# Two graph-network layers on one core: the residual sums of the output frame as two 512-wide operations behind the third clip, in place of four 256-wide ones between the second and the third

## The chip, the core and the metric

The kernel runs on one core of a Trainium2 chip. TensorE (PE) multiplies matrices, VectorE (DVE), ScalarE (ACT) and GpSimd (POOL) work on elements, SyncE (SP) starts most transfers; each has a queue of its own that it works off in order. The metric is the device time of one execution in microseconds (us), lower being better.

## The reference, cut to what matters

The input `x` holds 8 graphs of 2048 nodes with 256 features, in float32, and one 2048 x 2048 adjacency serves them all. Layer 0, which the change concerns, is

```python
h = jnp.maximum(_layernorm(x, axis=-1), 0.0)
q, k, v = h @ Wq.T + bq, h @ Wk.T + bk, h @ Wv.T + bv      # 4 heads of 64
scores = einsum('bhnd,bhjcd->bhnjc', q, kc) / sqrt(64)      # keys in 8 chunks of 256
scores = jnp.clip(scores, -10.0, 10.0)
scores = jnp.where(mask == 0, -10.0, scores)
attn = jax.nn.softmax(scores, axis=-1)                      # within each chunk
ctx = einsum('bhnjc,bhjcd->bhnd', attn, vc)                 # summed over chunks
out = ctx @ Wo.T + bo + h                                   # the residual sum
x = x + (layernorm(out) * gamma + beta)
```

Layer 1 is a graph attention layer on `relu(layernorm(x))`, with one softmax over all 2048 neighbours, and adds its relu to `x`. The change touches the line of the residual sum, `out = ctx @ Wo.T + bo + h`, and only the order and the shape in which its last addition is done.

## The kernel before, in words

**Tiling.** For each graph the queries are cut into 4 blocks of 512 (`NB`, index `nb`) and the keys into 8 chunks of 256 (`j`). A step of the attention is one pair (block, chunk): 32 steps a graph, 256 in all. Activations lie transposed, so a step's logits are [128 keys x 512 queries] tiles. The four heads are taken one after another in the order `ORDER`, index `o` from 0 to 3; heads that lie in the lower 64 rows of the array alternate with heads in the upper 64, so two half-arrays of 64 rows, each split into four column groups of 32, work side by side. Below they are called the two halves.

**The frame.** `begin(f)` and `end(f)` write out one frame, in which four steps overlap: the logits and clips of step f-1, most of the values and the sums of step f-2, the rest of the values, the inversion and the scaling of step f-3, and the first logits of step f. `logits` (L411) is the matrix product of keys and queries; `clip` (L451, DVE) reads a pair of banks of logits, clips them and applies the mask in one operation, and so frees the pair; `exponentials` (L460) is on ACT; `values` (L427) and `sums` (L439) are PE again; `scale` (L481, DVE) multiplies by the inverse sum into `prod`, and `gather` (L486, POOL) adds `prod` to `ctxT` by an accumulating DMA. The clips of o = 0 to 3 are called the first to the fourth; the first is in `begin`, the others in `end`.

**What sets the order.** `tc.manual_schedule` takes the order of the program as it is written, so an engine's queue is the order in which the Python calls are made. Between engines, semaphores hold back readers and writers of the same buffer. In PSUM there are two double banks `ps_s` for logits, two banks `ps_n` for values and two banks `ps_t`, taken in turns. So `logits(f-1, 3, ...)` needs the pair that the second clip of the same frame has freed, and `logits(f, 0, 0)` the pair that the third has freed.

**Work beside the attention.** `Between.beside` hands out the rest of the layer as pieces with a half-frame number n; even n go to `begin`, odd n to `end`. A piece has a kind that says where in the frame it is called. The pieces of the output projection of a finished block are at n = 8 and n = 9, that is, in one frame, which is called the output frame below. In `begin`, `output_tiled(0)` (kind `pe`) puts 32 matmul calls of 256 columns ahead of the logits of the second and third heads, and in `end` `output_tiled(1)` (kind `pe1`, L635) puts another 32 behind them. Together they fill two `ps_t` banks, `pp[0]` and `pp[1]`. The addition of the residual, `ps_t` plus `hn0` into `o4`, is then `take_tiles` (L650, kind `mid`): for i = 0 and 1 it adds 256 columns out of each of the two banks. `end` runs these pieces after the second clip and before the third. The bank `pp[0]` is then taken again by `sums(f-2, 1)` in the same frame. Pieces without a kind that belong to n = 8, among them `stats([0])` on `o4`, run after the third clip. There are 3 such blocks for each of 8 graphs, so 24 output frames; the fourth block of a graph takes another way (`output`, and `take` at L658).

**Two fp32 passes.** Each fp32 matmul call is recorded as two instructions: the logits make 256 x 4 x 2 x 4 = 8192 calls, and the profile counts 16384.

Of the kernel before, what the change touches and what calls it, by code (L numbers as in the profile page):

```python
# [8 lines left out]
F32 = mybir.dt.float32  # L9
# [4 lines left out]
ALU = mybir.AluOpType  # L14
# [3 lines left out]
P = 128  # L18
# [10 lines left out]
def gnn_two_layers(  # L29
# [18 lines left out]
    nc = tc.nc  # L48
    B, N, F = x.shape
# [6 lines left out]
    TB = NB // P  # L56
    NNB = N // NB
# [36 lines left out]
    work = ctx.enter_context(tc.tile_pool(name="work", bufs=2, reuse_waits="tile"))  # L94
# [64 lines left out]
    def first(piece):  # L159

        piece.kind = "first"
        return piece

    def pe(piece):

        piece.kind = "pe"
        return piece

    def pe1(piece):
        piece.kind = "pe1"  # L170
        return piece

    def mid_clips(piece):
        piece.kind = "mid"
        return piece


# [105 lines left out]
    def norm_tiles(tag, bufs):  # L283
        mv = small.tile([P, TB, 2], F32, tag="mv", name="mv")
        rn = small.tile([P, 2, TB], F32, tag=tag, name=tag, bufs=bufs)
        return mv, rn
# [94 lines left out]
    def fence(before, after):  # L381

        nop = nc.sync.nop()  # L383
        for x in before:
            tc.add_manual_dep(nop.ins, x.ins.name, SYNC, reason="both write one bank of PSUM")
        for x in after:
            tc.add_manual_dep(x.ins, nop.ins.name, SYNC, reason="both write one bank of PSUM")


    class Attention:  # L390
# [159 lines left out]
        def end(self, f, pieces=()):  # L550
            self.run(pieces, "first")
            if self.has(f - 1):
                self.clip(f - 1, 1)
            self.run(pieces, "pe1")
            self.run(pieces, "mid")
            if self.has(f - 1):
                self.clip(f - 1, 2)
            self.run(self.rest, None)
            if self.has(f - 1):
                self.exponentials(f - 1, 1)  # L560
                self.exponentials(f - 1, 2)
            if self.has(f - 2):
                made = {}
                for kt in range(KT):
                    for half, c in ((0, 1), (1, 0)):
                        made.setdefault(c, []).extend(self.values(f - 2, half, c, kt))
                for c in range(2):
                    self.before[f - 2, c] = made[c]
            if self.has(f - 1):
                self.logits(f - 1, 3, 0)  # L570
            if self.has(f - 2):
                sums = self.sums(f - 2, 1)
            if self.has(f - 1):
                self.logits(f - 1, 3, 1)
            if self.has(f):
                self.logits(f, 0, 0)
            self.run(pieces, None)
            self.run(pieces, "pe")
            if self.has(f - 2):
                fence(sums, self.sums(f - 2, 0))  # L580
            if self.has(f):
                self.logits(f, 0, 1)
            if self.has(f - 1):
                self.clip(f - 1, 3)
                self.add(f - 1, 0)
# [8 lines left out]
    class Between:  # L594
# [23 lines left out]
        def output_tiled(self, turn):  # L618
# [22 lines left out]
            for t2 in range(2) if turn else ():  # L641
                fence(self.made[t2], made[t2])
            self.made = made

        def take_tiles(self, i):
            if i == 0:
                self.o4 = work.tile([P, TB, F], F32, tag="o4", name="o4", bufs=1)
                self.mv, self.rn = norm_tiles("rn", 2 * NNB)
            for t2 in range(2):
                nc.vector.tensor_tensor(  # L650
                    self.o4[:, 2 * t2 + i, :], self.pp[t2][:, i * F:(i + 1) * F], self.hn0[t2][:, i, :], op=ALU.add
                )

        def take(self, t2):
            if t2 == 0:
# [90 lines left out]
        def beside(self):  # L746

            todo = {
                -3: [self.load],
                3: [lambda: self.residual(0)],  # L750
                4: [lambda: self.residual(1)],
                5: [lambda: self.bias(0)],
                6: [lambda: self.bias(1)],
                8: [pe(lambda: self.output_tiled(0)), lambda: self.stats([0]), lambda: self.beta(0)],
                9: [
                    pe1(lambda: self.output_tiled(1)), mid_clips(lambda: self.take_tiles(0)),
                    mid_clips(lambda: self.take_tiles(1)), lambda: self.stats([1]),
                ],
                10: [lambda: self.stats([2]), lambda: self.beta(1)],
                11: [lambda: self.stats([3])],  # L760
                12: [self.power],
                13: [self.shift],
                14: [lambda: self.scaled(range(TB))],
                15: [lambda: self.gamma(0)],
                16: [lambda: self.gamma(1)],
                18: [lambda: self.add(0)],
                20: [lambda: self.add(1)],
            }

            def at(n, *pieces):  # L770
                todo.setdefault(n, []).extend(pieces)

            if self.nb == NNB - 2:
                return todo
            at(22, lambda: self.stats1([0]))

            at(25, first(lambda: self.stats1([1, 2, 3])))
            at(26, self.power1)
            at(27, self.shift1)
            if self.nb == 1:  # L780
                at(28, lambda: self.norm1(0))
                at(29, lambda: self.norm1(1))
            return todo
# [225 lines left out]
    for b in range(B):  # L1009
# [3 lines left out]
        zero, low, mid, last = blocks  # L1013
# [271 lines left out]
```

The softmax here doesn't subtract the row's maximum and nothing guards it: scores larger than these inputs give would overflow.

## Time and profile before

| | |
|---|---|
| median of 3 runs | 3626.41 us (3624.73 to 3626.59) |
| the profiled execution's own time | 3624.46 us |
| its span | 3622.7 us |
| PE busy, by the page | 3587.4 us, 99% of the span |
| DVE busy | 2580.6 us, 71% |
| ACT busy | 1960.9 us, 54% |
| POOL busy | 1788.1 us, 49% |
| `take_tiles`, L650 on DVE | 96 operations, 34.0 us |
| granted TensorE clock | 0.998 |

Busy times are unions of the instructions of an engine. The ends of matmuls are modelled in the profile and not recorded, so PE's share says that matmuls were in flight and not that PE never waited; starts are recorded. PEld is the weight load of PE. In the lists of groups, the number after the bar is the busy time in us and the mean of one in ns, then the idle time of the engine just ahead of the group with what ended most of it. In a timeline, each row gives the start, the length, the engine, the line, the operation, the tiles, how many operations were merged into the row, and in brackets the idle time ahead of it.

### The profile page before, as it was taken

The numbers are of one execution on the slowest core, as the hardware profiler recorded it, in microseconds if no ns is written. First come the engines' busy times: TensorE is split into PE (matmuls) and PEld (weight loads), VectorE is DVE, ScalarE is ACT, GpSimd is POOL, SyncE is SP. The second block draws the span as 40 slices with busy tenths as digits, with TensorE's granted clock in tenths as the row PEclk, the third lists the DMA queues.
The fourth block names the chain that finished last, engine by engine and source line by source line (L and its number), as shares of the span: only waits on it lengthen the run. The fifth ranks groups of instructions, "written<-read, shape, count | busy, mean of one in ns | idle before, by whom it ended". The sixth has DMA issues, their size and how long they took to land.

```text
span 3622.7 us, 104823 instructions
## 1 busy us (share of the span) xinstructions
PE 3587.4 (99%) x46544; PEld 2202.7 (61%) x46544; DVE 2580.6 (71%) x3967; ACT 1960.9 (54%) x2975; POOL 1788.1 (49%) x1138
## 2 busy tenths in 40 slices
PE   8999999999999999999999999999999999999999
PEld 4444785547744577555775558744586455865568
DVE  5887577866777667786677766677576785757866
ACT  5677416774167732676326772367723677137650
POOL 0678016870178702786027850378503784047831
PEclk9999999999999999999999999999999999999999
DMA  6444213341133412343113432144322343114321
GB/s 223 114 109 100 49 56 84 84 107 35 64 81 83 107 35 68 84 96 83 53 50 84 104 74 62 48 85 99 71 61 59 78 96 73 53 48 92 75 60 44
DMA packets 149431, 283.62 MB, mean 78 GB/s; under 512 B 39664, under 2 KB 104944, under 8 KB 140784
## 3 DMA queue, kind: packets, MB, share of 16 engines
q0 software_dynamic: 32256, 117.45, 17.6%
q1 hardware_dynamic: 100080, 157.36, 13.5%
q8 instruction: 364, 5.96, 0.7%
q10 hardware_dynamic: 16640, 2.10, 0.4%
q14 instruction: 91, 0.75, 0.1%
HBM read 138.41 MB, written 21.02 MB: 44 GB/s over the span
## 4 chain that ended last, share of the span: by engine, by line
PE 96%; DMA 2%; ACT 1%; DVE 1%; issue 0%; POOL 0%; ACTq 0%; SPq 0%; DVEq 0%; POOLq 0%
PE ps_s L411 24%; PE ps_n L427 24%; PE ps_s L865 12%; PE ps_t L439 6%; PE ps_n L865 6%; PE ps_t L865 6%; PE ps_t L635 2%; PE ps_t L355 2%; PE ps_n L355 2%; PE ps_s L355 2%; PE ps_t L723 2%; PE ps_n L723 1%; PE ps_t L369 1%; PE ps_n L369 1%; PE ps_t L302 1%; DMA ctxT<-prod 1%
## 5 line engine op out<-in xcount | busy, mean ns | idle before, releaser
L466 POOL TENSOR_TENSOR both<-e 128x1024 f32<-128x1024 f32 x512 | 1217.8, 2406 | 641.1 <-PE ps_t L439 353.3
L451 DVE SCALAR_TENSOR_TENSOR e<-ps_s,bound 128x1024 f32<-128x1024 f32 x1024 | 1223.9, 1220 | 401.4 <-PE ps_s L411 398.6
L411 PE MATMUL ps_s<-q,k 64*32 64x512 f32 x16384 | 1435.0, 590 | 2.1 <-DVE e L451 2.1
L460 ACT ACTIVATE e<-e 128x1024 f32<-128x1024 f32 x1024 | 1050.5, 1050 | 524.8 <-DVE e L451 505.1
L427 PE MATMUL ps_n<-e,v 64*32 64x512 f32 x16384 | 1220.2, 590 | 2.7 <-ACT e L460 2.1
L427 PEld LDWEIGHTS ps_n<-e,v 64*32 64x32 f32 x16384 | 453.9, 107 | 476.4 <-issue 396.4
L411 PEld LDWEIGHTS ps_s<-q,k 64*32 64x32 f32 x16384 | 451.8, 106 | 472.0 <-issue 326.9
L883 POOL TENSOR_TENSOR x<-x,r 128x256 f32<-128x256 f32 x124 | 95.8, 773 | 1107.2 <-DVE rz L875 1000.7
L439 PE MATMUL ps_t<-both,ones 64*32 64x512 f32 x4096 | 534.7, 591 | 0.1
L865 PE MATMUL ps_s<-g,w 128*128 128x257 f32 x2048 | 448.5, 380 | 0.0
L865 PEld LDWEIGHTS ps_s<-g,w 128*128 128x128 f32 x2048 | 389.4, 190 | 56.5
L481 DVE TENSOR_TENSOR prod<-ps_n,rz 128x512 f32<-128x512 f32 x448 | 288.3, 685 | 159.3 <-PE ps_n L427 96.4
L848 DVE SCALAR_TENSOR_TENSOR w<-bound,w 128x1024 f32<-128x1024 int8 x256 | 313.7, 1225 | 8.7
L865 PE MATMUL ps_n<-g,w 128*128 128x257 f32 x1024 | 292.4, 382 | 0.0
L865 PE MATMUL ps_t<-g,w 128*128 128x257 f32 x1024 | 289.8, 380 | 0.0
L842 DVE TENSOR_SCALAR w<-src,cd 128x512 f32<-128x512 f32 x512 | 265.2, 560 | 10.7 <-ACT src L836 6.9
L471 ACT ACTIVATE rz<-ps_t 128x512 f32<-128x512 f32 x256 | 152.8, 597 | 175.7 <-PE ps_t L439 136.9
L486 POOL DMA_DIRECT2D ctxT<-prod x224 | 192.3, 859 | 57.7 <-DVE prod L481 55.2
L865 PEld LDWEIGHTS ps_n<-g,w 128*128 128x128 f32 x1024 | 192.8, 190 | 44.3 <-issue 17.6
L865 PEld LDWEIGHTS ps_t<-g,w 128*128 128x128 f32 x1024 | 193.8, 189 | 28.2
L275 ACT ACTIVATE krn<-mv,eps 128x4 f32<-128x4 f32 x32 | 9.5, 296 | 292.7 <-DVE mv L271 292.7
L439 PEld LDWEIGHTS ps_t<-both,ones 64*32 64x32 f32 x4096 | 115.2, 106 | 85.8 <-SPq L383 42.4
(126 smaller groups left out, 3005.0 us busy)
## 6 DMA issues: line engine op xcount, KB each, us to landing
ctxT<-prod POOLq DMA_DIRECT2D x224, 512.0 KB, 4.8
bound<-bound_d SPq DMA_DIRECT2D x62, 1024.0 KB, 5.7
xp<-in_x_dram SPq DMA_DIRECT2D x60, 512.0 KB, 5.7
rows<-in_adj_dram SPq DMA_DIRECT2D x32, 512.0 KB, 5.2
x<-in_x_dram SPq DMA_DIRECT2D x32, 512.0 KB, 4.6
out_dram<-x SPq DMA_DIRECT2D x31, 512.0 KB, 2.9
src<-source_d SPq DMA_DIRECT2D x24, 256.0 KB, 4.8
bound_d<-bound_part ACTq DMA_DIRECT2D x16, 128.0 KB, 4.4
```

The costliest lines, as they stand in the source:

```text
L355: nc.tensor.matmul(pp, w[:, di, do * P:(do + 1) * P], self.hT[nb][:, di, :], start=di == 0, stop=di == FC - 1,)
L411: nc.tensor.matmul(self.s[n, o][c * Q:(c + 1) * Q, kt, :], self.k[p][rows, at:at + Q], self.q[p][rows, nb * NB:(nb + 1) * NB], start=True, ...
L427: made.append(nc.tensor.matmul(self.num[n, c][h * Q:(h + 1) * Q, :], self.v[rows, j * KT + kt, at:at + Q], self.e[n, p][rows, i * KT + kt, :],
L439: nc.tensor.matmul(self.total[n][h * Q:(h + 1) * Q, :], ones[rows, :], self.both[n, h // 2][rows, h % 2, :], start=half == 1, stop=half == 0,)
L451: nc.vector.scalar_tensor_tensor(self.e[n, p][:, i * KT:(i + 1) * KT, :], self.s.pop((n, o)), -CLIP * SC, bounds[nb][:, j * KT:(j + 1) * K ...
L460: nc.scalar.activation(e, e, AF.Exp, scale=1.0 / SC)
L466: nc.gpsimd.tensor_tensor(self.both[n, p], e[:, 0], e[:, 1], op=ALU.add)
L481: nc.vector.tensor_tensor(dst[:, c, :], self.num.pop((n, c)), self.rz[n], op=ALU.mult)
L486: nc.gpsimd.dma_start(self.ctxT[nb], self.prod.pop(n), accum_op=ALU.add)
L842: nc.vector.tensor_scalar(w[:, i, :], self.src[nb], self.cd[:, 0, j:j + 1], self.cd[:, 1, j:j + 1], op0=ALU.mult, op1=ALU.max,)
L848: nc.vector.scalar_tensor_tensor(two, bounds1[nb][:, j - 1:j + 1, :], 0.0, two, op0=ALU.is_gt, op1=ALU.mult)
L865: nc.tensor.matmul(accs[t][:, 0:F + 1], w[:, i, t * P:(t + 1) * P], g[:, j, :], start=j == 0, stop=j == NT - 1,)
```

## The change

The four 256-wide additions between the second and the third clip become two 512-wide ones, one for each bank, and they are called after the third clip. The method `take`, which the last block of a graph used already, does them; `take_tiles` goes. Matmuls, banks, ACT, POOL and SP keep their work and their order.

```diff
-    def mid_clips(piece):
-        piece.kind = "mid"
+    def after_clips(piece):
+        piece.kind = "after"
         return piece
...
             self.run(pieces, "pe1")
-            self.run(pieces, "mid")
             if self.has(f - 1):
                 self.clip(f - 1, 2)
+            self.run(pieces, "after")
             self.run(self.rest, None)
...
-        def take_tiles(self, i):
-            if i == 0:
-                self.o4 = work.tile([P, TB, F], F32, tag="o4", name="o4", bufs=1)
-                self.mv, self.rn = norm_tiles("rn", 2 * NNB)
-            for t2 in range(2):
-                nc.vector.tensor_tensor(
-                    self.o4[:, 2 * t2 + i, :], self.pp[t2][:, i * F:(i + 1) * F], self.hn0[t2][:, i, :], op=ALU.add
-                )
-
...
                 9: [
-                    pe1(lambda: self.output_tiled(1)), mid_clips(lambda: self.take_tiles(0)),
-                    mid_clips(lambda: self.take_tiles(1)), lambda: self.stats([1]),
+                    pe1(lambda: self.output_tiled(1)), after_clips(lambda: self.take(0)),
+                    after_clips(lambda: self.take(1)), lambda: self.stats([1]),
                 ],
```

The method that is now called in the output frame, unchanged:

```python
        def take(self, t2):
            if t2 == 0:
                self.o4 = work.tile([P, TB, F], F32, tag="o4", name="o4", bufs=1)
                self.mv, self.rn = norm_tiles("rn", 2 * NNB)
            nc.vector.tensor_tensor(
                self.o4[:, 2 * t2:2 * t2 + 2, :], self.pp[t2].rearrange("p (i f) -> p i f", i=2),
                self.hn0[t2], op=ALU.add,
            )
```

## The prediction

> **What bounds the kernel now.** First the page, for the shares of the engines.
>
> ```profile
> PE 3587.4 (99%) x46544; PEld 2202.7 (61%) x46544; DVE 2580.6 (71%) x3967; ACT 1960.9 (54%) x2975; POOL 1788.1 (49%) x1138
> ```
>
> PE bounds it and no other engine is near. But the ends of matmuls are modelled, so a short stall of PE shows only in its starts. Second, the groups of DVE with their shapes kept apart, for the operation that goes and the one that comes.
>
> ```profile
> L650 DVE TENSOR_TENSOR o<-ps_t,hn 128x256 f32<-128x256 f32 x96 | 34.0, 416 | 26.0 <-PE ps_t L635 26.0
> ...
> L658 DVE TENSOR_TENSOR o<-ps_t,hn 128x512 f32<-128x512 f32 x8 | 5.5, 690 | 12.1 <-PE ps_t L613 12.1
> ```
>
> L650 is `take_tiles`: DVE stands idle ahead of it for 26.0/24 = 1.1 us in each output frame, until the last output matmul is done. L658 is `take`, as the fourth block runs it. Third, the timeline of DVE through the output frame of graph 0, block 1.
>
> ```profile
> 249.29 1.23 DVE L451 SCALAR_TENSOR_TENSOR e<-ps_s,bound 128x1024 f32<-128x1024 f32 x1 [0.49 <-PE ps_s L411]
> 251.62 1.42 DVE L650 TENSOR_TENSOR o<-ps_t,hn 128x256 f32<-128x256 f32 x4 [1.10 <-PE ps_t L635]
> 252.95 1.21 DVE L451 SCALAR_TENSOR_TENSOR e<-ps_s,bound 128x1024 f32<-128x1024 f32 x1
> ```
>
> The rows are the second clip, the four additions and the third clip, which ends at 254.16. It stands behind the 1.10 us of idleness and the 1.42 us of additions only because DVE's queue is in that order. Fourth, PE in the same stretch.
>
> ```profile
> 253.01 0.61 PE L439 MATMUL ps_t<-both,ones 64*32 64x512 f32 x4
> 253.34 0.62 PE L411 MATMUL ps_s<-q,k 64*32 64x512 f32 x4
> ...
> 253.44 0.61 PE L439 MATMUL ps_t<-both,ones 64*32 64x512 f32 x4
> 253.77 1.08 PE L411 MATMUL ps_s<-q,k 64*32 64x512 f32 x8
> ...
> 254.22 0.13 PEld L411 LDWEIGHTS ps_s<-q,k 64*32 64x32 f32 x5 [0.73 <-DVE e L451]
> ```
>
> Each row x4 fills the four column groups of one half; within a half the next follows 0.43 us later. The half that did sums at 253.01 and 253.44 is due with `logits(f, 0, 0)` at 253.87. It starts at 254.22, 0.06 us after the third clip's end, and its weight load names that clip: 0.35 us lost. Is it made up? The starts of the first sums of four successive frames answer that.
>
> ```profile
> 241.84 0.61 PE L439 MATMUL ps_t<-both,ones 64*32 64x512 f32 x4
> ...
> 253.01 0.61 PE L439 MATMUL ps_t<-both,ones 64*32 64x512 f32 x4
> ...
> 261.11 0.61 PE L439 MATMUL ps_t<-both,ones 64*32 64x512 f32 x4
> ...
> 268.83 0.61 PE L439 MATMUL ps_t<-both,ones 64*32 64x512 f32 x4
> ```
>
> The distances are 11.17, 8.10 and 7.72. An undisturbed frame takes 7.725 (9 groups in each half, two passes each, 18 x 0.429). The output matmuls add 16 groups of 256 columns in each half, 16 x 0.215 = 3.43, so 11.16 is due for the first distance, and 0.02 is lost there. The second has no matmul beyond a plain frame's and is 8.093 by the trace's unrounded starts: 0.368 lost for good. In all 21 output frames of graphs 1 to 7, and in this one, the loss lies between 0.367 and 0.369.
>
> **What the Trainium skill says.** "Perfetto Trace Analysis", Identifying the Most-Contended Engine: the busy share of matmuls is no good measure of PE's headroom. The trace agrees: the page's 99% contain the 0.368. "TensorE: Matmul & The Clock Gate", Part 3, The mechanism: matmuls run in strict first-in, first-out order, so one held up holds those behind it. The trace agrees in part: the other half's sums, next in the queue, slipped by 0.05. "VectorE: DVE Perf Modes", The TRN2 errata, prices an operation from PSUM at 120 cycles plus its elements at 0.96 GHz; I estimate 392 ns for 256 and 658 ns for 512. The rows above say 416 and 690, and I use those.
>
> **The change part by part.**
>
> *Additions.* Four at 416 ns go; with overlapping ends they take 1.42 us as one row. Two at 690 ns come; two such products of L481 follow each other in 1.29 us. That saves 0.13 us of DVE, 24 x 0.13 = 3 us in all, worth nothing by itself: DVE waits for PE in this frame. Their issue, their semaphores and every DMA stay as they are.
>
> *Third clip.* It moves ahead of the additions. Its logits were finished at 249.75 (last start 249.14 plus 0.61). Pairs of clips take 2.36 us in other frames, so it runs from 250.43 to 251.65, in the idle 1.10 us and a little beyond, 2.5 us earlier. `logits(f, 0, 0)` then keeps its slot at 253.87 with 2.2 us to spare, and the 0.35 us are gone. The exponential behind the clip moves from 254.28 to about 251.75, when ACT is idle.
>
> *Additions behind the clip.* The last output matmul ends at 251.48 and DVE is free at 251.65, so `take(0)` starts at about 251.65 where `take_tiles` started at 251.62. It ends by 252.34, `take(1)` by 252.95. `sums(f-2, 1)`, due at 253.01, takes over the bank `pp[0]`, read last by `take(0)`: 0.6 us to spare. Were it held until `take(1)`, 252.95 plus 0.06 would still just do. Behind them `stats` and the fourth clip come 1 us earlier, also with no one waiting.
>
> *Gross gain.* 22 frames x 0.368 = 8.10. The other two, in graph 0, lie beside other extra matmuls; there I read 0.32 and 0.35 off the late starts. Sum: 8.77 us.
>
> *What the gather takes back.* There is a second chain close behind PE: sums, `add` on POOL, `gather`, its DMA, then `scale`, which reuses `prod`.
>
> ```profile
> 1090.87 0.86 POOL L486 DMA_DIRECT2D ctxT<-prod  x1
> 1096.97 1.29 DVE L481 TENSOR_TENSOR prod<-ps_n,rz 128x512 f32<-128x512 f32 x2 [1.34 <-DMA ctxT<-prod]
> ...
> 1097.71 0.15 PEld L427 LDWEIGHTS ps_n<-e,v 64*32 64x32 f32 x8 [0.92 <-DVE prod L481]
> ```
>
> Here `scale` waited 1.34 us for the DMA and PE then waited for `scale`. Counted from a frame's first sums, the gather is issued at 7.085, its DMA lands 4.5 to 6 us later, and `scale` starts at landing plus 0.12, or at 11.80 if the DMA is early. Over the trace's plain frames, the next frame loses the time by which `scale` starts after 12.37, to 0.01 us where nothing else disturbs it. In the frame that holds the stall, this limit lies 0.37 later, at 12.73; the change moves it back to 12.37, and its gather 0.095 earlier. With the landings recorded for those frames, five of 24 cross it: by 0.14, 0.25, 0.03, 0.04 and 0.30, together 0.76 us. If none is late this term is 0; if these frames lose what plain frames do on average (13.6 us in some 120, 0.11 each), it is 2.7. I take 0.76 and keep 0 and 2.7.
>
> *Sum.* 8.77 - 0.76 = 8.0 us, with ends 6.1 and 8.8. Against the profiled execution: 3624.46 - 8.0 = 3616.4. The median of the runs is 1.95 above that execution, so I put the time at 3626.41 - 8.0 = 3618.4 us, a fall of 0.22%.
>
> **The rivals.**
>
> *The gather takes most of it.* The wait moves from the clip to the DMA. For it: 38.8 us of waits of `scale` on this DMA, and landings that scatter. Against it: 19 of the 24 recorded landings would be early enough, and the transfers beside them don't change. With 1.5 to 6 us taken back the gain is 2.8 to 7.25, the time 3619.2 to 3623.6.
>
> *Nothing comes of it.* The 0.35 us turn out to be a lead that one half must give up anyway, and another wait closes the frame. For it: the other half slips by 0.05 only, and its start within the frame is nearly as before. Against it: the frame distance itself is 0.368 too long and never made up, and plain frames, with their clips together, run at 7.725. Time: 3625 to 3627.
>
> *Slower: `sums` waits for its bank.* PE's first-in, first-out queue would stand at `sums(f-2, 1)` until `take(0)` has read `pp[0]`. For it: the addition now stands behind a clip of 1.21 us. It begins to cost where `take(0)` ends after 252.95, and loses against the old order from 253.3 on, that is, if the third clip starts about 1 us later than forecast, for a wait that I don't see. If `take(0)` ended at 253.7, PE would lose 0.75 a frame in place of 0.365: 24 x 0.385 = 9.2 us, 3635.6. Against it: clips follow each other at once in other frames, with the same buffers.
>
> **How the numbers follow.** Forecast with a take-back up to 1.5 us (3617 to 3619.2): 0.68. Gather takes more: 0.20. Nothing: 0.07. Slower: 0.05. The bound of 0.2%, about what a measurement of this kernel can tell from no change, is 7.25 us, a time of 3619.2; so faster has the first case, 0.68; no change the second and third, 0.27; slower 0.05. The range takes the forecast, the bounds of the gather's term and the runs' own scatter of 2 us: 3615.5 to 3622.5. It leaves out the last two cases and the tail of the gather's.
>
> **What would show it.** The second and third clips in one row of 2.36 us, with both additions behind them and no wait of more than 0.1 for L635. No weight load of L411 that waits 0.7 us for L451 in these frames. First sums 11.16 to 11.18 and then 7.725 apart where 8.093 stood, in about 19 of 24; where more, `scale` waits for the DMA of `ctxT`. The prediction is wrong if a weight load of L439 waits for the new additions, if the second distance stays near 8.09, or if late transfers of the gather pile up in these frames.

## The result, and the profile after

The changed kernel takes 3618.7 us (median of 20 runs, 3611.44 to 3624.58), the kernel before 3626.5 us (median of 20, 3622.49 to 3631.91). The ratio is 0.9978, with a 95% interval of 0.9972 to 0.9984. The forecast was 3618.4 us, a fall of 0.22%. The profiled execution took 3618.74 us, its span 3616.9 us.

The page of the changed kernel, its line of engines:

```profile
PE 3579.6 (99%) x46544; PEld 2222.8 (61%) x46544; DVE 2583.1 (71%) x3919; ACT 1960.0 (54%) x2975; POOL 1787.0 (49%) x1138
```

DVE has 48 instructions fewer and is no less busy: 2583.1 us against 2580.6. What fell is PE, with the same 46,544 matmuls. The groups of DVE by shape have the new additions in one row with the old use of `take`; 48 of its 56 are new:

```profile
L649 DVE TENSOR_TENSOR o<-ps_t,hn 128x512 f32<-128x512 f32 x56 | 36.2, 683 | 10.4 <-PE ps_t L613 10.4
```

The 26.0 us of idleness that L650 had ahead of it are gone; what is left belongs to the fourth blocks (L613). The timeline of DVE through the same output frame as in the prediction:

```profile
252.15 2.36 DVE L451 SCALAR_TENSOR_TENSOR e<-ps_s,bound 128x1024 f32<-128x1024 f32 x2 [0.49 <-PE ps_s L411]
254.42 1.28 DVE L649 TENSOR_TENSOR o<-ps_t,hn 128x512 f32<-128x512 f32 x2
...
257.31 1.23 DVE L451 SCALAR_TENSOR_TENSOR e<-ps_s,bound 128x1024 f32<-128x1024 f32 x1 [0.53 <-PE ps_s L411]
```

The second and third clips are one row, the two additions follow with no wait, and the fourth clip now waits 0.53 us for its matmuls; before, its logits lay finished while it stood in VectorE's queue. PE and its weight load in the same stretch:

```profile
256.25 0.62 PE L439 MATMUL ps_t<-both,ones 64*32 64x512 f32 x4
256.63 0.66 PE L411 MATMUL ps_s<-q,k 64*32 64x512 f32 x8
256.68 0.14 PEld L411 LDWEIGHTS ps_s<-q,k 64*32 64x32 f32 x4 [0.29 <-issue]
...
257.06 0.61 PE L439 MATMUL ps_t<-both,ones 64*32 64x512 f32 x4
257.10 0.62 PE L411 MATMUL ps_s<-q,k 64*32 64x512 f32 x4
```

The eight matmuls at 256.63 are both halves together: the first pass of `logits(f, 0, 0)` follows the sums of 256.25 in its slot of 0.43 us. Its weight load names no clip any more: "issue" means that it waited for nothing that the profile shows. Of the starts of the sums I take the first of four frames again:

```profile
244.64 0.62 PE L439 MATMUL ps_t<-both,ones 64*32 64x512 f32 x4
...
255.82 0.62 PE L439 MATMUL ps_t<-both,ones 64*32 64x512 f32 x4
...
263.54 0.62 PE L439 MATMUL ps_t<-both,ones 64*32 64x512 f32 x4
...
271.27 0.62 PE L439 MATMUL ps_t<-both,ones 64*32 64x512 f32 x4
```

The distances are 11.18, 7.72 and 7.73. By the unrounded starts, the second is 7.725 in every one of the 21 output frames of graphs 1 to 7, where it was 8.09.

**Where the time went.** I set the 255 distances between first sums of the two profiled executions side by side. In the 24 frames after an output frame, 8.75 us fell away. In the frames next to those, 1.3 us came back. All other frames together are 0.65 us shorter, so the stretch from the first sums to the last became 8.05 us shorter. The two spans differ by 5.8 us only, because the changed kernel reached its first sums 3.7 us later in this execution, long before the first output frame, and made up 1.4 us after the last sums. The runs of one kernel scatter by more than that, so the medians stand for the size and the distances for the cause.

### The profile page after: what moved, and what is told of

The parts are those of the page before. It is cut to its first block, busy times and chain, and to the rows that moved or that the text cites. A ratio compares the mean times of both kernels' runs of the same rounds, so it can differ in the third digit from the quotient of the medians.

```text
span 3616.9 us, 104751 instructions
## 1 busy us (share of the span) xinstructions
PE 3579.6 (99%) x46544; PEld 2222.8 (61%) x46544; DVE 2583.1 (71%) x3919; ACT 1960.0 (54%) x2975; POOL 1787.0 (49%) x1138
## 4 chain that ended last, share of the span: by engine, by line
PE 97%; DMA 1%; DVE 1%; ACT 1%; issue 0%; POOL 0%; ACTq 0%; SPq 0%; DVEq 0%; POOLq 0%
PE ps_s L411 24%; PE ps_n L427 24%; PE ps_s L856 12%; PE ps_t L439 6%; PE ps_n L856 6%; PE ps_t L856 6%; PE ps_t L635 2%; PE ps_t L355 2%; PE ps_n L355 2%; PE ps_s L355 2%; PE ps_n L714 2%; PE ps_t L714 1%; PE ps_t L369 1%; PE ps_n L369 1%; PE ps_t L302 1%; DMA ctxT<-prod 1%
## 5 line engine op out<-in xcount | busy, mean ns | idle before, releaser
L466 POOL TENSOR_TENSOR both<-e 128x1024 f32<-128x1024 f32 x512 | 1216.3, 2402 | 639.3 <-PE ps_t L439 340.8
L451 DVE SCALAR_TENSOR_TENSOR e<-ps_s,bound 128x1024 f32<-128x1024 f32 x1024 | 1225.0, 1221 | 412.1 <-PE ps_s L411 410.2
L411 PE MATMUL ps_s<-q,k 64*32 64x512 f32 x16384 | 1412.0, 590 | 2.1 <-DVE e L451 2.1
L427 PE MATMUL ps_n<-e,v 64*32 64x512 f32 x16384 | 1206.8, 590 | 4.1 <-ACT e L460 2.2
L486 POOL DMA_DIRECT2D ctxT<-prod x224 | 192.3, 859 | 57.8 <-DVE prod L481 55.5
L472 ACT ACTIVATE rz<-rz 128x512 f32<-128x512 f32 x256 | 161.4, 630 | 8.2
```

Source lines behind the costliest of these rows:

```text
L411: nc.tensor.matmul(self.s[n, o][c * Q:(c + 1) * Q, kt, :], self.k[p][rows, at:at + Q], self.q[p][rows, nb * NB:(nb + 1) * NB], start=True, ...
L427: made.append(nc.tensor.matmul(self.num[n, c][h * Q:(h + 1) * Q, :], self.v[rows, j * KT + kt, at:at + Q], self.e[n, p][rows, i * KT + kt, :],
L451: nc.vector.scalar_tensor_tensor(self.e[n, p][:, i * KT:(i + 1) * KT, :], self.s.pop((n, o)), -CLIP * SC, bounds[nb][:, j * KT:(j + 1) * K ...
L466: nc.gpsimd.tensor_tensor(self.both[n, p], e[:, 0], e[:, 1], op=ALU.add)
L486: nc.gpsimd.dma_start(self.ctxT[nb], self.prod.pop(n), accum_op=ALU.add)
```

## The experiments

Times are compared with runs of the kernel before on the same chip. "The distance" is that from the first sums of the output frame to those of the next, 8.093 us before, 7.725 us after the change.

**The order alone.** The four old additions, moved.

```diff
-            self.run(pieces, "mid")
             if self.has(f - 1):
                 self.clip(f - 1, 2)
+            self.run(pieces, "mid")
```

> The kernel before with the four 256-wide additions kept and only moved behind the third clip. Theory (the place of the third clip in VectorE's queue is the whole cause): the clip runs 2.5 us earlier, the third addition has read the bank pp[0] some 0.3 us before the sums are due, so the frame after each output frame falls from 8.093 to 7.725 us in at least 20 of the 21 cases of graphs 1 to 7, and the time falls as with the whole change, ratio to before 0.9970 to 0.9985. Rival (the 512-wide shape is the cause): distances stay at 8.09 and the ratio is within 0.0008 of 1.

Measured: 3618.15 us, ratio 0.9981 (0.9973 to 0.9989); the distance is 7.725 in all 21. VectorE's timeline of the same frame:

```profile
250.42 2.36 DVE L451 SCALAR_TENSOR_TENSOR e<-ps_s,bound 128x1024 f32<-128x1024 f32 x2 [0.49 <-PE ps_s L411]
252.69 1.41 DVE L650 TENSOR_TENSOR o<-ps_t,hn 128x256 f32<-128x256 f32 x4
```

The order is enough for the distance. The bank `pp[0]` comes free later than with the wide additions, because the third of the four still reads it: in most frames this addition ends 0.375 us before the sums start, and in one output frame of graph 0 it was too late and the sums slipped by 0.19 us.

**The shape alone.** Two 512-wide additions in the old place.

```diff
-    mid_clips(lambda: self.take_tiles(0)), mid_clips(lambda: self.take_tiles(1)),
+    mid_clips(lambda: self.take(0)), mid_clips(lambda: self.take(1)),
```

> The kernel before with two 512-wide additions in place of the four, left between the second and the third clip. Theory: the additions take 1.29 in place of 1.42 us, so the third clip ends 0.13 us earlier and the late logits lose 0.21 in place of 0.345 us; the frame after each output frame takes 7.95 to 7.98 us, 24 x 0.13 = 3 us less in all, some of it taken back by the gather: ratio 0.9990 to 1.0000. Rival (shape is the cause): 7.725 us and a ratio near 0.9978.

Measured: 3623.62 us, ratio 0.9992 (0.9984 to 1.0000); the distance is 7.966 to 7.969. VectorE's timeline of the same frame:

```profile
249.88 1.29 DVE L658 TENSOR_TENSOR o<-ps_t,hn 128x512 f32<-128x512 f32 x2 [1.10 <-PE ps_t L635]
251.09 1.22 DVE L451 SCALAR_TENSOR_TENSOR e<-ps_s,bound 128x1024 f32<-128x1024 f32 x1
```

The wait of 1.10 us is still there; the clip starts 1.21 us after the first addition where it started 1.33 us after it. By the unrounded records the clip ends 0.127 us earlier, and the distance shortened by 0.126. By the distances the shape has a third of the gain where it stands ahead of the clip. The interval of its ratio touches 1.

**Split by bank, and split by columns.** Both leave half of the additions ahead of the third clip and put half behind it; they differ in which half.

```diff
 # by bank
-    mid_clips(lambda: self.take_tiles(0)), mid_clips(lambda: self.take_tiles(1)),
+    mid_clips(lambda: self.take(0)), behind(lambda: self.take(1)),
 # by columns
+    mid_clips(lambda: self.take_tiles(0)), behind(lambda: self.take_tiles(1)),
 # in end(), behind the third clip
+            self.run(pieces, "behind")
```

> take(0), 512 wide, stays between the second and the third clip, take(1) goes behind the third. VectorE still stands idle 1.1 us ahead of take(0), and the clip ends at 253.5 on the scale of the frame shown of the kernel before, where the logits are due at 253.87. Theory (only a clip that ends after the due time minus 0.06 costs anything): nothing is lost, frames of 7.725 us, ratio as with the whole change, 0.9970 to 0.9985. Rival (the wait for the output matmuls ahead of a clip is itself what costs): between a third and two thirds of the gain, distances of 7.85 to 8.0 us.

> The same number of elements ahead of the third clip, but cut the other way: the first 256 columns of both banks ahead of it, the last 256 of both behind. The third clip ends as early as in the split by bank, but the bank pp[0] is read last at about 253.83 on the scale of the frame shown, where the sums that take it over are due at 253.01. Theory with the rival of the prediction (the sums' bank): the first sums start 0.85 to 0.9 us late, the distance into the output frame's sums grows from 11.18 to about 12.05 us, the next one is 7.725; net 24 x (0.88 - 0.37) = 12 us slower than before, ratio 1.0025 to 1.0040. Rival (only the clip's place counts): as with the whole change, 0.9978.

By columns: 3637.14 us, ratio 1.0039 (1.0026 to 1.0052), slower as expected. The distance into the output frame's sums is 12.144 (11.18 before), the next one 7.722. In the trace (L655 are the additions, L443 the sums):

```profile
252.64 0.75 DVE L655 TENSOR_TENSOR o<-ps_t,hn 128x256 f32<-128x256 f32 x2
...
253.20 0.63 PE L443 MATMUL ps_t<-both,ones 64*32 64x512 f32 x4 [0.44 <-DVE o L655]
```

PE stands still for the addition that reads the last columns of `pp[0]`, the first of the two in the row. This is the prediction's slower rival, brought about: it needs the bank to be read late, and its price is 0.966 us a frame. I had expected 0.85 to 0.9. By the unrounded records the sums start 0.146 us after that addition's end (0.145 to 0.147 in all 24 frames), and I had allowed 0.06, which is what the logits need after a clip.

By bank: 3619.09 us, ratio 0.9984 (0.9977 to 0.9990). The time agrees with the expectation, the distance does not: 7.851 to 7.855, not 7.725, which is the edge of the rival's range. The third clip did come in time. The loss is two clips further on:

```profile
255.50 2.32 DVE L455 SCALAR_TENSOR_TENSOR e<-ps_s,bound 128x1024 f32<-128x1024 f32 x2
...
257.88 0.58 PEld L415 LDWEIGHTS ps_s<-q,k 64*32 64x32 f32 x20 [0.49 <-DVE e L455]
```

These are the fourth clip and the first one of the next frame in one row with no wait ahead of them, ending at 257.82, and logits that wait for the first clip. VectorE works without a break from `take(0)` on, so the 1.1 us that it stood idle ahead of `take(0)` are missing two clips later. That is a limit that I had not seen. The next run tests it.

**Split by bank, with one pair of statistics later.**

```diff
-    behind(lambda: self.take(1)), lambda: self.stats([1]),
+    behind(lambda: self.take(1)),
...
-                12: [self.power],
+                12: [lambda: self.stats([1]), self.power],
```

> The split by bank again, with one pair of statistics operations (stats of the second tile, 0.54 us of VectorE) taken out of the output frame and done three half-frames later. The split by bank lost 0.128 us a frame although its third clip came in time; its trace shows VectorE busy without a break from take(0) on, and logits of the next frame waiting 0.49 us for that frame's first clip. Theory now (a third limit: VectorE must be through the fourth and the next first clip in time): with 0.54 us less ahead of the fourth clip the distance of 7.853 falls to 7.725 us, and the ratio to before is that of the whole change, 0.9970 to 0.9985. Rival (the wait ahead of the clip costs through something else, ScalarE's or the logits' order): 7.85 us stays.

Measured: the distance is 7.725 in all 21, so the 0.128 us were VectorE's lateness. The time is a miss: 3629.22 us, ratio 1.0010 (1.0004 to 1.0017). The statistics cost more where they were put. Of the 14 distances that begin two frames after those sums, in the first and second blocks of graphs 1 to 7, ten were 7.725 without the move; these are 7.87 to 7.98 with it. The third blocks' are longer by 0.29 or more, and the distances that follow lose another 0.3 or more in most blocks. So an operation of 0.54 us is free in one frame and costs in another.

**Banks swapped.** `take(1)` ahead of `take(0)`.

> The whole change with take(1) ahead of take(0), so that the bank that the sums take over, pp[0], is read last. take(0) then ends at about 252.95 on the scale of the frame shown of before, and the sums are due at 253.01. Theory: free 0.06 us after its reader, it is just in time; distances of 11.18 to 11.22 and 7.725 us, time within 0.05% of the whole change. Rival (the release needs more than 0.06 us): the sums slip by 0.1 us or more and the first distance exceeds 11.28.

Measured: 3614.51 us, ratio 0.9972 (0.9963 to 0.9982), 0.06% from the ratio of the whole change, with overlapping intervals; distances 11.178 and 7.725. `take(0)`, now last, ends at 254.19, its sums start in their slot:

```profile
253.51 0.68 DVE L650 TENSOR_TENSOR o<-ps_t,hn 128x512 f32<-128x512 f32 x1
...
254.37 0.61 PE L439 MATMUL ps_t<-both,ones 64*32 64x512 f32 x4
```

Between them lie 0.175 us. The split by columns needed 0.146, so, if the wider addition needs the same, the swapped order has 0.03 us to spare and the changed kernel's own has 0.6 more.

**Without the gather.** In both kernels the accumulating transfer is left out.

```diff
             if j > 0:
-                nc.gpsimd.dma_start(self.ctxT[nb], self.prod.pop(n), accum_op=ALU.add)
+                self.prod.pop(n)
```

> The kernel before without the accumulating transfers: the products of chunks 1 to 7 are computed and left out of the sum over chunks, so only chunk 0 enters the context. Theory (the gather is a second chain that sets 15 us of losses in the kernel before): VectorE no longer waits for a transfer ahead of the scaling, the frame after each output frame still takes 8.09 us, the frames that lost 0.1 to 1 us to late landings take 7.725; ratio to before 0.9940 to 0.9965. Rival (late landings are only seen beside losses of another cause): ratio above 0.998.

> The whole change without the accumulating transfers, the same part of the sum left out. Theory: without the gather nothing is taken back, so the change is worth the gross 8.8 us between this run and the one before it without transfers (0.24%, 0.20 to 0.28% by the medians), and its total stands at a ratio to before of 0.9915 to 0.9940; every distance of graphs 1 to 7 after an output frame is 7.725. Rival (the 0.37 us is a lead that another wait takes once transfers are gone): the two runs without transfers lie within 0.1%.

Measured: 3598.44 us (ratio 0.9927, 0.9914 to 0.9941) without the change, 3590.99 us (0.9911, 0.9897 to 0.9925) with it. Both are faster than expected (0.9940 to 0.9965 and 0.9915 to 0.9940), the second by little. Frame by frame, the attention of the kernel before lost 16.5 us less, about the 15 us that its gaps ahead of the scaling had promised; 6.9 us more lie in the long stretches between graphs, 5.1 of them in one graph, which the expectation left out. Between the two runs without transfers the medians differ by 7.45 us, or 0.21%, at the low end of what was expected. In their traces every frame after an output frame is 0.37 shorter with the change and nothing comes back in the frames next to those: 9.1 us in the 24 frames, two of which differ by 0.1 more. Other frames are 1.2 us longer in sum with the change, so the stretch from the first sums to the last is 7.9 us shorter; what lengthened those was not looked into.

**The gather in halves.** The traces say that late landings cost more than the whole change gained, so I tried to relieve them: two buffers of 2 KB in place of one of 4 KB, with a transfer each.

```diff
-                self.prod[n] = work.tile([P, 2, NB], F32, tag="prod", name="prod", bufs=1)
+                self.prod[n, c] = work.tile([P, NB], F32, tag="prod", name="prod", bufs=2)
...
-                nc.gpsimd.dma_start(self.ctxT[nb], self.prod.pop(n), accum_op=ALU.add)
+                nc.gpsimd.dma_start(self.ctxT[nb][:, c, :], self.prod.pop((n, c)), accum_op=ALU.add)
```

> The whole change with the gather cut in two: each half of the product has a buffer of its own in the same 4 KB, and each is added to the context by a transfer of 256 KB of its own, the first issued where the one transfer was, the second 0.86 us later on GpSimd. Theory (late landings of the gather are what is left to lose, 17 us in the trace of the changed kernel): the first half lands earlier than the whole did, VectorE's scaling of it waits less, frames with losses of 0.1 to 1 us become rare; 8 to 16 us less than the whole change, ratio to before 0.9935 to 0.9960. Rival (the transfers share their engines and GpSimd pays 0.86 us more per frame): the second half lands too late or GpSimd's additions do, nothing gained or lost, ratio 0.9975 or more.

> The changed kernel once more, beside the run with the halved gather on the same chip: 0.9970 to 0.9985 of before by either theory.

The changed kernel beside it: 3616.03 us, ratio 0.9979 (0.9973 to 0.9986). The halved gather: 3697.05 us, ratio 1.0196 (1.0182 to 1.0210), far worse than either theory. Its DMA issues and two of its waits:

```profile
ctxT<-prod POOLq DMA_DIRECT2D x448, 256.0 KB, 4.2
```

```profile
POOL both L466 <- PE ps_t L439: 242.9, 136, 3.7
...
DVE prod L481 <- DMA ctxT<-prod: 105.0, 73, 4.2
```

The 4.2 us are a median over two kinds of transfer. By the trace's records the first halves land 3.4 us after their issue and the second halves, issued 0.6 us behind the first, 4.9 us after theirs (medians of 224 each); the whole took 4.8. So the first half of the product is free 1.4 us earlier than the whole was, and the second 0.9 us later, counted from the first issue. `scale` waits 105.0 us in all, where the changed kernel has 40.9, and 104.7 of them are for the second half. POOL, which pays for each issue, lost a third of its slack (340.8 us of waiting for PE in the changed kernel, 242.9 here). The granted clock was 0.993 in this profile against 0.998. With the 2.8 us for each 0.001 that the last section reads off the runs of the kernel before, 14 of the 73 us that this run lies above the kernel before may go with it, an estimate beyond the clocks that those runs had. How the rest splits between the two waits is open.

## Why the prediction was right, point by point

- *The late third clip costs PE 0.368 us in each output frame.* Right. Moving the additions alone takes it away, and in the shape alone a shift of the clip's end by 0.127 us shows as 0.126 in the distance.
- *The clip moves into the idle 1.10 us.* Right: one row of 2.36 us.
- *The 0.13 us that the wider additions save are worth nothing.* Right behind the clip: the order alone, with four additions, has the same distances as the whole change. Ahead of the clip they are worth 3 us, as the step on the clip implies and that sentence did not say.
- *`take(0)` frees `pp[0]` with 0.6 us to spare.* Right, by two errors that cancel: the sums need 0.146 us after their reader and not 0.06, and `take(0)` ended 0.773 us before them in most frames and not 0.67. That leaves 0.63. The prediction's "would still just do" for `take(1)` was tried by the swapped order, which fits by 0.03.
- *`stats` and the fourth clip come 1 us earlier, with no one waiting.* Right that no one waits; the sizes are about 1.3 us for `stats` and 0.7 for the fourth clip, which is then held by its own logits.
- *Gross gain 8.77 us.* The traces have 8.75. In graph 0 two readings missed in opposite ways: the two frames that were read as 0.32 and 0.35 shortened by 0.367 and 0.285, the second of them mixed with other losses.
- *The time of 3618.4 us.* The median lies 0.3 us from it, which is luck in part: the interval of the ratio is 2.2 us wide to each side.
- *The gather takes back 0.76 us, 0 to 2.7.* Right in kind, and within the range: 1.3 us in six frames of graphs 1 to 7. In five of them, together 1.04 us, the rule behind it held to 0.01 us; `scale` started 12.616, 13.001 and 12.447 us after the first sums in three frames, the rule of 12.37 gives 0.25, 0.63 and 0.08, and the next frames lost 0.251, 0.636 and 0.082. In the sixth `scale` started in time, 12.11 us after the first sums, so its 0.256 us have another cause, which is open. The landings of one execution are a sample: where I reused the recorded ones, other frames were late. The largest loss, 0.636, is one landing after 5.8 us. The prediction's sign for it, longer second distances in some frames, was misplaced: all 21 of these are 7.725, and by its own rule the loss falls in the distance after.
- *Rivals.* That nothing comes of it is excluded by the order alone. That the sums wait for their bank is a real mechanism and was not met here; the split by columns shows it. That the gather takes most of it did not happen in this profile.

What the prediction did not have is the limit on the fourth and first clips. It did not matter, because moving all additions behind the third clip also ends the idleness ahead of them; with half of them left in place, as in the split by bank, a third of each frame's gain is lost (0.128 of 0.368).

## What to carry to other kernels

In an in-order queue, an operation that must wait for another engine should stand behind those that are ready and whose result the bounding engine needs next; look for a wait in the middle of the queue of an engine that is not busy. Measure what it costs by the distances between starts on the bounding engine, since its busy share does not show it. Then ask which buffer the moved operation frees and when its next owner is due, and which second chain runs close behind and takes part of the gain.

## What the runs showed of the hardware

- A reader's release is not one number: where PE was held, logits start 0.055 us after a clip's end (L451, before and in the shape alone), sums 0.146 us after the addition's (L655, split by columns), both from the records of starts and ends. Why they differ is open.
- An accumulating transfer of 512 KB lands 4.8 us after its issue (changed kernel). Cut in two, the first 256 KB land after 3.4 us and the second, issued 0.6 us behind, after 4.9 us (medians). So the last byte is no earlier, and GpSimd pays for another issue, 395.3 us in all where it paid 192.3.
- The five runs of the kernel before without the gather lie within 2.4 us, the four of the changed kernel without it within 5.9, the 41 of the kernel before with it, beside the first experiments, within 16. The numbers of runs differ, so this does not show that the landings make the scatter. Part of it goes with the granted clock: over the 100 runs of the kernel before beside the experiments, the mean is 3620.4 us at a clock of 1.000 (7 runs), 3623.0 at 0.999 (48), 3626.1 at 0.998 (33), 3628.8 at 0.997 (11) and 3630.0 at 0.996 (1), or about 2.8 us for each 0.001.
